# Slot numbers stored in a node's row, own places for rows, one-hots and staging, and x in host-laid tiles

## Chip, cores and metric

The kernel runs on one core of one Trainium2 chip. The metric is device time in microseconds (us) of that core for one launch, inputs in HBM. Times are medians of a kernel's runs. A ratio is the mean time of one kernel's runs over that of the kernel before in the same rounds, so it is not quite the ratio of the medians quoted beside it. There is one profile of each kernel, so marks and rates compared below are of single executions; only the times and ratios come from several.

## The reference, cut to what matters

Four graph layers run one after the other on x (8 batches, 2048 nodes, 64 features). The change concerns the first one, a hypergraph attention layer with 64 hyperedges, and one set of loads in the stage after it.

```python
def _L0_gnn_ref(x, H, adj, ...):
    h = x @ W
    alpha = softmax(where(H.T > 0, leaky_relu(h @ a_node), NEG))        # node -> hyperedge
    agg = einsum('ben,bnf->bef', alpha, h)                              # the 64-row "table"
    beta = sigmoid((h @ a_gn)[:, None, :] + (agg @ a_ge)[:, :, None])
    all_he = elu(beta[..., None] * h[:, None] + (1 - beta[..., None]) * agg[:, :, None])
    deg = maximum(adj.sum(-1), 1.0)[:, None]
    industry = einsum('nm,bmf->bnf', adj / deg, x @ W_ind)              # the products "u"
    coefs1 = softmax(where(H > 0, attn_scores(elu(agg)), NEG))          # hyperedge -> node
    g = einsum('bne,benf->bnf', coefs1, all_he)
    # ... g and industry are then combined, and three more layers follow
```

A node belongs to a few hyperedges only. The kernel sorts the nodes by that number and works in "slots": slot s of a row tile (128 sorted nodes) is each node's s-th hyperedge, picked from the table by a one-hot matmul.

## The kernel before: the parts concerned

Layer 0, in the program's order. Names: `hrow` is a gathered row, `hrh` and `hrl` are its two halves, `o` is a one-hot, `ps` holds the scores of a row tile's slots, from which VectorE makes the factors `R` and `co`; `pz` is row plus table entry of one slot, `du` are the degrees, `v0h` and `v0l` the halves of a piece of x. SyncE and ACT issue the loads and stores, GpSimd the gathers. The parts that the argument needs:

```python
def split(pool, src, tag, bufs, shape):          # f32 as two fp32r halves
    ...
    nc.scalar.copy(hi, src)
    nc.vector.tensor_tensor(lo, src, hi, ALU.subtract)

def load_adj(t):                                 # adj tile t: 2 x 512 KB
    for k in range(2):
        a = pa.tile([P, HN], F32, tag="a", name="a", bufs=4)
        nc.sync.dma_start(a, adj_t[t * P:(t + 1) * P, cols(k, HN)])
        if t < NT - XT: nc.gpsimd.tensor_copy(adj[t][:, cols(k, HN)], a)    # 12 tiles
        else:           nc.scalar.copy(adj[t][:, cols(k, HN)], a)           # the last 4
...
for t in range(NT):                              # rows of H in sorted order, for the slot numbers
    nc.gpsimd.indirect_dma_start(out=hs[:, t, :], in_=h_ne, in_offset=order[:, t])
# ... row tiles h -> hs_hbm (two staging rows), agg, degree passes du += ones.T @ adj[t],
# ... slot numbers from hs, table tab2, ts2; then all of adj is cast, then:

def begin(t):                                    # row tile t of the slot phase
    hrow = pl.tile([P, BF + 8], F32, tag="hrow", bufs=2)
    nc.gpsimd.indirect_dma_start(out=hrow, in_=hs_hbm, in_offset=order[:, t])
    both = split(pb, hrow[:, 0:BF], "hr", 2, [P, BF])
    # one-hots on GpSimd, ps matmuls, R, rs, co on VectorE
for t in range(NT):
    for s in range(S):
        # 3 matmuls into pz (PSUM); begin(t + 1) at s == 0
        fill(8)                                  # 8 of the 512 product matmuls "u"
        nc.vector.tensor_tensor(z, z, R[:, s], ALU.mult)                    # z lies in PSUM
        y = pl.tile([P, B, F], F32, tag="y", bufs=2)                        # y lies in SBUF
        nc.scalar.activation(y, z, AF.Exp, bias=-1.0)
        nc.vector.scalar_tensor_tensor(y, z, 1.0, y, op0=ALU.max, op1=ALU.min)
        nc.vector.tensor_tensor(y, y, cb, ALU.mult)                         # "y times co"
        nc.gpsimd.tensor_tensor(acc, acc, y, ALU.add)                       # s > 0
# inside the products, once: a block of 16 one-row matmuls "pdc" turns the degrees into a column
```

## Time and profile before

| | before |
|---|---|
| time, three runs | 2225.7 us median (2225.62 to 2230.62) |
| layer 0: start to the first gather of the next stage | 297.5 us |
| first row gather | 101.3 us |
| first product matmul | 112.6 us |
| last product matmul ends | 293.1 us |

The span splits at the next stage's first gather, which waits for layer 0's last product. Everything behind it is the same program in both kernels but for the loads of x.

### The profile page before, as it was taken

Reading aid. Unit: us, or ns where it says so; the run is one execution under the profiler, and the core shown is the slowest. Engines: PE = TensorE matmul, PEld = TensorE weight load, DVE = VectorE, ACT = ScalarE, POOL = GpSimd, SP = SyncE. Lnnn points to the kernel's source line nnn. Section 1 sums busy time; section 2 is a strip of 40 time slices with the busy share of each in tenths; the row PEclk is TensorE's granted clock in tenths of the full one; section 3 lists DMA queues with packets and bytes.
Section 4 is the critical chain, followed back from the end, with each engine's and each line's share of the span. In section 5 each row is a group of like instructions: output and inputs, shape, how many; then the busy total and the mean of one; then the engine's idle time right before and its main releaser. Section 6 shows DMA issues by size and latency. Waiting matters only on the chain.

```text
span 2227.2 us, 19810 instructions
## 1 busy us (share of the span) xinstructions
PE 1993.1 (89%) x7318; PEld 1289.3 (58%) x7318; DVE 1139.1 (51%) x1900; ACT 338.3 (15%) x584; POOL 551.0 (25%) x499
## 2 busy tenths in 40 slices
PE   7799978888759999799999999999986989999994
PEld 4488745555644444375456456447434777777873
DVE  5479956666532222216864773782784344331312
ACT  1322323222111111010010001001000011111110
POOL 5457466564323323200110110110010001010202
PEclk7889989999969999999999999999998999999997
DMA  8723334322210000000000000000001223200000
GB/s 263 237 66 91 95 91 107 83 70 63 76 46 0 19 19 19 19 24 5 10 5 3 10 8 1 10 8 3 8 8 32 76 72 85 62 19 1 20 1 21
DMA packets 99306, 103.26 MB, mean 46 GB/s; under 512 B 63088, under 2 KB 63136, under 8 KB 99008
## 3 DMA queue, kind: packets, MB, share of 16 engines
q1 hardware_dynamic: 73248, 83.09, 12.8%
q0 software_dynamic: 4064, 9.10, 1.7%
q10 hardware_dynamic: 21888, 9.70, 1.6%
q8 instruction: 60, 0.98, 0.2%
q14 instruction: 46, 0.38, 0.1%
HBM read 75.59 MB, written 26.28 MB: 46 GB/s over the span
## 4 chain that ended last, share of the span: by engine, by line
PE 63%; DVE 12%; DMA 12%; POOL 7%; issue 4%; ACT 2%; SPq 0%; ACTq 0%; POOLq 0%; DVEq 0%
PE py L967 18%; PE u L171 17%; PE u L914 10%; PE u L527 9%; DMA fcav<-in_adj_t 7%; POOL ln_r L155 3%; PE pz L171 2%; DVE fcav L1061 2%; PE pf L171 1%; PE pr L171 1%; DMA x<-x_hbm 1%; DVE ln_v L151 1%; DVE ln_c L145 1%; DVE ln_m L143 1%; ACT r L149 1%
## 5 line engine op out<-in xcount | busy, mean ns | idle before, releaser
L967 PE MATMUL py<-wp,xg 128*128 128x512 f32 x1024 | 448.5, 597 | 8.5 <-DVE fcav L972 5.8
L967 PEld LDWEIGHTS py<-wp,xg 128*128 128x128 f32 x1024 | 193.6, 191 | 254.4 <-issue 216.4
L171 PE MATMUL u<-adj,hi 128*128 128x512 f32 x768 | 256.5, 415 | 0.0
L171 PE MATMUL u<-adj,lo 128*128 128x512 f32 x768 | 246.5, 400 | 1.1 <-DVE lo L1026 1.1
L914 PE MATMUL u<-pt,xn 128*128 128x512 f32 x512 | 227.5, 603 | 8.3 <-DVE u L923 7.1
L972 DVE TENSOR_TENSOR fcav<-py,emb_n 128x512 f32<-128x512 f32 x256 | 177.0, 691 | 52.0 <-PE py L967 37.5
L975 POOL TENSOR_TENSOR r<-r,bias 128x256 f32<-128x256 f32 x32 | 23.3, 729 | 636.0 <-DVE r L973 636.0
L973 DVE TENSOR_REDUCE r<-fcav 128x32 f32<-128x512 f32 x256 | 175.4, 685 | 8.1
L914 PEld LDWEIGHTS u<-pt,xn 128*128 128x128 f32 x512 | 97.3, 193 | 130.2 <-issue 114.7
L527 PE MATMUL u<-adj,vh 128*128 128x512 f32 x512 | 158.3, 408 | 15.4 <-ACT vh L166 11.6
L171 PEld LDWEIGHTS u<-adj,hi 128*128 128x128 f32 x768 | 143.2, 190 | 40.8 <-issue 11.5
L171 PEld LDWEIGHTS u<-adj,lo 128*128 128x128 f32 x768 | 144.6, 190 | 35.4 <-DVE lo L1026 1.6
L527 PE MATMUL u<-adj,vl 128*128 128x512 f32 x512 | 152.1, 398 | 0.0
L155 POOL TENSOR_TENSOR ln_r<-ln_e,neg_half 128x8 f32<-128x8 f32 x64 | 106.1, 1658 | 174.9 <-DVE ln_e L153 166.9
L908 DVE TENSOR_SCALAR pt<-pt 128x512 f32<-128x512 f32 x64 | 49.1, 784 | 172.8 <-ACT pt L907 171.3
L1045 POOL TENSOR_TENSOR r<-r,xn 128x512 f32<-128x512 f32 x16 | 20.4, 1275 | 418.9 <-DVE r L1044 418.9
L527 PEld LDWEIGHTS u<-adj,vh 128*128 128x128 f32 x512 | 96.2, 189 | 45.7 <-ACT vh L166 13.1
L912 POOL TENSOR_TENSOR acc<-acc,pt 128x512 f32<-128x512 f32 x60 | 79.6, 1327 | 162.6 <-DVE pt L908 159.8
L527 PEld LDWEIGHTS u<-adj,vl 128*128 128x128 f32 x512 | 96.4, 189 | 22.1 <-issue 0.7
L1061 DVE SCALAR_TENSOR_TENSOR fcav<-fcav,adj 128x512 f32<-128x512 f32 x64 | 44.5, 695 | 117.6 <-DMA fcav<-in_adj_t 117.1
L149 ACT ACTIVATE r<-ln_c 128x512 f32<-128x512 f32 x64 | 40.4, 631 | 288.4 <-DVE ln_c L145 274.8
L709 POOL DMA_INDIRECT gn<-gs_hbm,rank x64 | 69.7, 1088 | 34.7 <-issue 14.2
(316 smaller groups left out, 2774.3 us busy)
## 6 DMA issues: line engine op xcount, KB each, us to landing
a<-in_adj_t SPq DMA_DIRECT2D x32, 512.0 KB, 5.9
fcav<-in_adj_t SPq DMA_DIRECT2D x64, 256.0 KB, 2.8
x_hbm<-r SPq DMA_DIRECT2D x20, 256.0 KB, 2.3
hs_hbm<-st ACTq DMA_DIRECT2D x16, 260.0 KB, 5.4
xt<-in_x_t SPq DMA_DIRECT2D x16, 256.0 KB, 5.4
u_hbm<-ut SPq DMA_DIRECT2D x16, 256.0 KB, 2.7
gs_hbm<-acc SPq DMA_DIRECT2D x16, 256.0 KB, 2.0
ut<-u_hbm SPq DMA_DIRECT2D x16, 256.0 KB, 3.2
```

Source lines behind the costliest of these rows:

```text
L149: nc.scalar.activation(r, xc, AF.Square)
L155: nc.gpsimd.tensor_tensor(rstd, vare, neg_half[:, :groups], ALU.pow)
L171: tc.keep_in_program_order(nc.tensor.matmul(*args, **kw))
L527: nc.tensor.matmul(u[c], lhsT=half[:, j, :], rhs=adj[t][:, cols(c)], start=t == 0 and i == 0, stop=ends and not own,)
L709: nc.gpsimd.indirect_dma_start(out=gn[:, j, :], out_offset=None, in_=g_rows, in_offset=bass.IndirectOffsetOnAxis(ap=rank4[:, p, c * JT + j ...
L908: nc.vector.tensor_scalar(pt, pt, 1.0, None, op0=ALU.max)
L912: nc.gpsimd.tensor_tensor(acc, acc, pt, ALU.add)
L914: nc.tensor.matmul(u[p], lhsT=xn[p][:, t, :], rhs=pt, start=t == 0, stop=t == NT - 1)
L967: nc.tensor.matmul(py.rearrange("p o d -> p (o d)"), lhsT=xg[b][:, q, cols(j, P)], rhs=wp[:, q, cols(k)], start=q == 0, stop=q == 1,)
L972: nc.vector.tensor_tensor(pr, py, e_b, ALU.mult)
L973: nc.vector.tensor_reduce(r[:, j, b, cols(k, OH)], pr, AX.X, ALU.add)
L1061: nc.vector.scalar_tensor_tensor(a, a, 1.0, adj[t][:, cols(k)].bitcast(F32), op0=ALU.mult, op1=ALU.not_equal, accum_out=left[:, t, k:k + 1],)
```

## The change

The intent: no gathers of H, for the slot numbers are computed in node order and travel as 64 more columns of each row; no waits of rows and reciprocals for adj's staging memory, for they get places of their own; row gathers after eleven of the sixteen adj tiles; the `lo` halves of x on GpSimd, to unload VectorE; and one x load where two with short pieces were. Cut to its core:

```diff
-    def split(pool, src, tag, bufs, shape):
+    def split(pool, src, tag, bufs, shape, eng=nc.vector):
-        nc.vector.tensor_tensor(lo, src, hi, ALU.subtract)
+        eng.tensor_tensor(lo, src, hi.bitcast(F32) if eng is nc.gpsimd else hi, ALU.subtract)
...
+    def staged(name):                            # shared by adj and x, four of 256 KB
+        return hy.tile([P, JT, P], F32, tag="x", name=name, bufs=4)
+    def load_adj(t):
+        for c in range(NCH):
+            a = staged("a").rearrange("p t f -> p (t f)")
+            nc.sync.dma_start(a, adj_t[t * P:(t + 1) * P, cols(c)])
+            tc.keep_in_program_order(nc.gpsimd.tensor_copy(adj[t][:, cols(c)], a))
...
+    HROW = BF + 8 + E
+    EARLY = 11
+        for c in range(NCH):                     # ahead of the small weights on ACT's queue
+            nc.scalar.dma_start(m_en[c], h_en[:, cols(c)])
-        for t in range(NT - XT):
+        for t in range(EARLY):
             load_adj(t)
...
+        # 16 small matmuls pcm, then the slot numbers of all nodes
+        nc.vector.tensor_tensor(slot, pcm, m_n, ALU.mult)
-        for t in range(NT):
-            nc.gpsimd.indirect_dma_start(out=hs[:, t, :], ..., in_=h_ne, ...)
...
-            st = pa.tile([P, BF + 8], F32, tag="st", name="st", bufs=2)
+            st = pa.tile([P, HROW], F32, tag="st", name="st", bufs=4)
+            nc.scalar.copy(st[:, BF + 8:], slot[:, t, :])
...
     def load_x(dst, p, c):
-        for b in range(2): ... eng.dma_start(dst[:, :, b * F:(b + 1) * F], x[2 * p + b, ...])
+        nc.sync.dma_start(dst, x_n[p, c])
...
-                part[c] = split(pb, xc.pop((p, c)), f"v{c}", 1, [P, JT, P])
+                part[c] = split(pb, xc.pop((p, c)), f"v{c}", 1, [P, JT, P], nc.gpsimd)
...
+        fetch_rows(0)                            # gathers; hrow in pool hy, three of them
+        fetch_rows(1)
+        for t in range(EARLY, EARLY + 2):
+            load_adj(t)
+        slots(0)                                 # pslot transpose, 12 one-hots on GpSimd
+        for t in range(EARLY + 2, NT):
+            load_adj(t)
         now = begin(0)
+        slots(1)
...
-                fill(8)
+                fill(4 if t == 0 and s < 6 else 8)
```

The last degree passes became filler between the slots of row tile 0, and products without slots follow at the end.

## The prediction

> **What bounds the kernel now.** I read the page first, then the chain of waits from 0 to 320 us, the waits from 60 to 140 us, the table of windows, and the timeline from 0 to 132 us and from 284 to 330 us. The change touches only layer 0 (0 to about 297 us) and, through the loads of x, the stage after it (297 to 640 us). The rest stands as it was, so the prediction is a sum over layer 0.
>
> Layer 0 has two halves. Until about 112 us the kernel loads adj (16.8 MB), computes rows and the one-hot table, and counts degrees. From 112 to 293.5 us TensorE runs 512 products `u` with 57 attention slots `pz` put between them. The chain of waits over the seam:
>
> ```profile
> 94.40 4.22 DMA a<-in_adj_t
> 98.65 1.04 ACT adj L253
> 99.69 0.92 ACT inv_row L505
> 100.61 0.70 issue
> 101.31 6.49 DMA hrow<-hs_hbm,order
> 107.84 2.04 DMA xc<-in_x
> 110.29 0.66 DVE R L630
> 111.58 1.24 PE pz L171 x2
> 113.44 0.69 DVE v0l L167
> 114.18 0.79 PE u L171
> ```
>
> The first row gather starts only at 101.31, when the last adj tile is cast and the degrees are copied, though the rows were written by about 79 us. Only then are rows gathered, x loaded, one-hots made and halves split, one after the other: 94 to 114 us is a string of waits. The waits from 60 to 140 us say the same:
>
> ```profile
> POOL hrow L613 <- ACT inv_row L505: 19.7, 1, 19.7
> DVE R L627 <- DMA xc<-in_x: 16.2, 1, 16.2
> ACT hrh L166 <- DMA hrow<-hs_hbm,order: 8.7, 2, 6.3
> ```
>
> GpSimd stands still for 19.7 us and VectorE for 16.2 us. (The releaser named for `R` is doubtful: the last `ps` matmul ends at 109.77 and `R` starts at 109.87.) The built program's wait lists explain it: the places of `hrow` and `R` are those of adj's staging buffers, so both wait for all eight last adj loads.
>
> The table of windows (us of the window, then PE, PEld, DVE, ACT, POOL busy, clock, DMA share, GB/s):
>
> ```profile
> 60.00:80.00 20.00, 15.22 (x60) 9.07 (x61) 15.01 (x35) 3.24 (x12) 12.29 (x12) 0.75 0.92 323
> 100.00:120.00 20.00, 13.56 (x35) 9.72 (x35) 8.17 (x21) 5.52 (x9) 14.04 (x22) 0.52 0.61 139
> 112.00:120.00 8.00, 7.47 (x20) 5.59 (x20) 6.10 (x15) 1.63 (x3) 4.38 (x6) 0.50 0.73 167
> 160.00:180.00 20.00, 20.00 (x91) 16.42 (x90) 19.85 (x39) 5.74 (x10) 13.31 (x14) 1.00 0.39 109
> 240.00:265.00 25.00, 21.45 (x95) 16.81 (x94) 24.96 (x46) 7.47 (x13) 9.56 (x8) 0.99 0.26 85
> ```
>
> Before 80 us the DMA engines are the bound (share 0.92 at 323 GB/s). From 160 us TensorE and VectorE are both full, and from 240 to 265 us VectorE alone is: TensorE has 3.6 us of gaps there.
>
> **What the Trainium skill says.** "DMA: Bandwidth & Descriptors", Anatomy of one DMA, gives a fixed cost of about 2 us a transfer that does not shrink with size. The trace agrees: the 256 KB loads of layer 3 land in 2.8 us (median). So half-size staging buffers, still four, hold less in flight. The same page, Specifications, wants at least 512 B a piece; here 63,088 of 99,306 packets are under that. "GPSIMD Engine Reference", section 3.1, puts a two-input elementwise operation on GpSimd at 1.96 times VectorE; here `acc` takes 1.294 us against 0.682, a factor of 1.9. "TensorE: Matmul & The Clock Gate", Part 1, says that the clock is halved after idling; here it is 0.50 from 112 to 120 us and eight `u` matmuls take 3.61 us, against 1.83 later.
>
> **The change, part by part.**
>
> Slot numbers. Gone are 16 gathers of H rows on GpSimd (median 0.96 us, 15.4 us, alternating with the adj casts between 32 and 52 us), VectorE's waits for them (9.9 us), 16 transposes, 4 ACT copies and 4 multiplies. In their place come 16 small matmuls and one multiply before row tile 0, which delay its matmuls to about 15 us (7.7 before), 64 columns more in each row, and a transpose and two ACT copies per tile later. The steady pace of row tiles was 2.2 us (`ex` at 31.49, 33.61, 35.86); before, it was lost to H waits and to the wait for the two staging rows (ACT 16.7 us behind `hs_hbm`). With four staging rows and no H gathers I take 2.2 us: the order is ready near 33 us as now, then 13 tiles, so the last row is issued at about 62 and lands near 67 us.
>
> adj. It now comes in 64 loads of 256 KB through four buffers, all cast on GpSimd (half of 1.04 us each). Estimate of the pace: 2.0 us fixed, 0.75 of transfer (256 KB at 350 GB/s, from the 70 to 80 us window, 351), 0.55 cast, 0.3 semaphores, with queueing 1.05 us a load, and 1.15 while rows are written. That is 4.2 to 4.7 us a tile. From the first at about 22 us, tile 10 is cast at about 70 us. The program places the first two row gathers after tile 10, so both conditions meet: gather at G = 69.
>
> From G on, by the order of the instructions on each engine: rows land at G+6.5; ACT takes them before it goes on with the table (`hrh` 0.62, `tab` 0.62, `hrh`, `het`), then `pf`, tanh, four degree passes' worth of tiles, `pse`, `ts`: table ready at G+14; one-hots 12 x 0.59 = 7.1 to G+22; first `z` on VectorE at G+23.6 = 92.6, against 112.84. But GpSimd casts tile 13 only after those 12 one-hots; then 5 more, tile 14 (its loads wait for the casts of 13), tile 15: cast at about G+33. Only then do the x loads get the four buffers: landed G+36. `v0h` on ACT, two row gathers and an `acc` go ahead on GpSimd, then `v0l` (1.3 us): G+38.4 = 107.4, against 114.2. Meanwhile 7 slots are done at VectorE's pace of 3 x 0.685 = 2.05 us, and the degrees run in their gaps.
>
> The products. TensorE's remaining work from there: 510 x 0.2287 = 116.6; 50 slots x 0.69 = 34.5; 40 `ps` at about 0.13 = 5.2; `pdc` 4.6, `pinv` 2.4, transposes 2.5; sum 165.8. Before it was 168 for 179.3 us of span; the difference was the cold clock (about 5.5 us until 129) and VectorE gaps (about 4.5). VectorE's remaining work after: 50 x 2.05 + 14 x 1.25 + 14 x 0.69 + 16 x 0.69 = 141 us, the 16 `lo` splits (11 us) having gone to GpSimd, which has some 125 us of work for this stretch. So TensorE alone is the bound; I add 2 us of gaps. End: 107.4 + 165.8 + 2 = 275.2, against 293.5: 18.3 us less. The tail is 59 products without slots; the next stage cannot start in it, because its first gather waits for the last product's store in both programs.
>
> x in host-laid tiles. 32 loads, in two pieces each with 256 B runs, become one each with 2 KB runs; ACT loses 16 issues of about 0.46 us in the next stage. DMA share there is 0.24 to 0.40 and the chain runs through arithmetic and waits on x1; I give it 1.5 us.
>
> Sum: 2225.7 - 18.3 - 1.5 = about 2206.
>
> **The rivals.** (1) The in-order queues give the gain back. GpSimd now carries every adj cast, the gathers and the one-hots, and the x buffers are adj's own. If adj comes at 5.3 us a tile (198 GB/s), tile 10 falls at 78 us, the first product at 116, and only the slots done early and the warmer clock are gained: about 2216. For it: only 1 MB in flight, and ACT's table work stands behind the gathers. Against it: the old H gathers are out of that queue. (2) VectorE stays the bound: then moving 11 us from it and starting 20 us earlier gives the whole 20 to 30 us, about 2198. For it: 19.85 of 20 us busy at 160 us; against it: its remaining 141 us lie well under TensorE's 166. (3) The transfers were hidden anyway: adj's bytes still set the first product and nothing moves, 2222. Against it: 94 to 114 us is a chain of latencies, not of bandwidth (139 GB/s from 100 to 120 us).
>
> **Range and chances.** The biggest doubts are G (plus or minus 6 us, one for one) and the gaps of the products (plus or minus 5). That gives 2195 to 2217 for 8 in 10. Faster by over 2% needs 2181, 25 us beyond my sum and some 44 us out of a stage with about 20 us of seam and 12 us of lost pace: 5%. Slower by over 2%: 1%.
>
> **What would show it.** Right: first row gather at 63 to 76 us; first `z` at 87 to 99; `v0l` of the first product at 101 to 114; last product at 268 to 283; VectorE below 90% between 160 and 240 us with TensorE full; no waits for `hs`. Wrong in step one if tile 10 is cast after 78 us; wrong in the handover if the gather is early and the product late; wrong in the pace if the span from the first to the last product is not 165 to 172 us; wrong in the last part if the stage from 297 to 640 us shifts by over 4 us against layer 0's end.

## More of the kernel before

One more line of the table of windows belongs here, because the prediction did not use it. Its columns are the window in us, its length, then busy time of TensorE, weight loads, VectorE, ACT and GpSimd (with counts), granted clock, DMA share and GB/s:

```profile
24.00:78.00 54.00, 41.41 (x187) 26.50 (x187) 34.08 (x90) 7.23 (x30) 37.02 (x37) 0.76 0.85 279
```

Over the whole stretch in which adj comes in and rows go out, the DMA engines moved 279 GB/s, less than the 323 GB/s of its last part.

## The result, and the profile after

The changed kernel takes 2236.55 us (2236.23 to 2237.39, 4 runs) against 2228.16 us (2225.62 to 2231.14, 4 runs) of the kernel before: ratio 1.0038, 95% interval 1.002 to 1.0055. It is slower by a little, within the 2% that count as the same, and outside the predicted range of 2195 to 2217.

| mark, us | before | predicted | after |
|---|---|---|---|
| first row gather | 101.31 | 69 | 80.97 |
| first z on VectorE | 112.84 | 92.6 | 104.40 |
| last adj tile cast | 99.7 | 102 | 114.6 |
| first product matmul | 112.6 | – | 118.8 |
| first product with v0l | 114.18 | 107.4 | 119.9 |
| last product matmul ends | 293.1 | 275.2 | 301.0 |
| next stage's first gather | 297.5 | – | 305.65 |
| end of span | 2227.2 | – | 2235.6 |

So the gather came 20 us earlier and the products began 6 us later. Behind layer 0 the two kernels took 1929.7 and 1929.95 us. The table of windows of the changed kernel, in the stretches that answer to those shown of before:

```profile
24.00:78.00 54.00, 42.34 (x214) 27.67 (x214) 35.53 (x101) 8.40 (x42) 25.50 (x42) 0.94 0.85 280
96.00:104.00 8.00, 5.62 (x16) 4.39 (x17) 1.16 (x4) 0.52 (x2) 7.22 (x14) 0.51 0.00 1
112.00:120.00 8.00, 7.65 (x30) 5.55 (x29) 5.28 (x9) 3.88 (x7) 6.50 (x8) 0.92 0.77 246
160.00:180.00 20.00, 19.59 (x91) 15.67 (x89) 18.51 (x31) 6.60 (x15) 14.40 (x14) 1.00 0.30 90
240.00:265.00 25.00, 21.74 (x97) 16.76 (x96) 24.59 (x46) 9.31 (x20) 16.34 (x16) 1.00 0.23 78
```

Three things are to be seen. From 24 to 78 us the DMA engines move 280 GB/s, as before. From 96 to 104 us they move next to nothing (1 GB/s), with three adj tiles not yet in place. And from 160 us VectorE is still at 93 to 98% although 11 us of work were taken from it, and TensorE has gaps again at 240 us.

The waits from 60 to 140 us (us in total, times, longest) answer to those of before; the chain that ended last has no piece in this stretch in this trace:

```profile
POOL adj L212 <- DMA a<-in_adj_t: 14.6, 12, 2.9
...
DVE R L647 <- PE ps L172: 9.1, 2, 7.8
ACT hrh L167 <- DMA hrow<-hs_hbm,order: 8.3, 2, 7.6
```

The 19.7 us that the gather waited for adj's end are gone, as intended, and `R` no longer waits for a load. In their place stand waits for adj's loads and for the `ps` matmuls, which wait for one-hots.

What GpSimd does in that DMA pause, from its timeline (start, length, line, operation, count, and in brackets the idle time before and what ended it):

```profile
80.97 1.05 POOL L616 DMA_INDIRECT hrow<-hs_hbm,order  x1 [0.28 <-DMA a<-in_adj_t]
...
88.46 2.58 POOL L212 CAST adj<-a 128x512 fp32r<-128x512 f32 x4 [2.88 <-DMA a<-in_adj_t]
95.35 7.02 POOL L633 TENSOR_SCALAR o<-slot 128x128 fp32r<-128x128 bf16 x12 [4.30 <-ACT slot L629]
102.43 2.29 POOL L212 CAST adj<-a 128x512 fp32r<-128x512 f32 x4
104.68 2.73 POOL L633 TENSOR_SCALAR o<-slot 128x128 fp32r<-128x128 bf16 x5
107.47 2.81 POOL L212 CAST adj<-a 128x512 fp32r<-128x512 f32 x4
111.15 1.24 POOL L212 CAST adj<-a 128x512 fp32r<-128x512 f32 x2 [0.87 <-DMA a<-in_adj_t]
113.38 1.27 POOL L212 CAST adj<-a 128x512 fp32r<-128x512 f32 x2 [0.98 <-DMA a<-in_adj_t]
```

It waits 4.3 us for the slot numbers of row tile 0, makes twelve one-hots in 7 us, and only then casts adj tiles 13 to 15. The four staging buffers are full meanwhile, so nothing is loaded.

VectorE's groups from 120 to 300 us (line, operation, shapes, count, busy us, mean ns, idle before), before and then after:

```profile
L654 DVE TENSOR_TENSOR pz<-pz,R 128x512 f32<-128x512 f32 x56 | 38.0, 685 | 0.5 <-PE pz L171 0.5
L663 DVE TENSOR_TENSOR y<-y,co 128x512 f32<-128x512 f32 x41 | 30.2, 744 | 0.1
L167 DVE TENSOR_TENSOR hrl<-hrow,hrh 128x512 fp32r<-128x512 f32 x14 | 12.3, 881 | 0.0
```

```profile
L694 DVE TENSOR_TENSOR y<-y,co 128x512 f32<-128x512 f32 x39 | 36.8, 946 | 0.5
L685 DVE TENSOR_TENSOR pz<-pz,R 128x512 f32<-128x512 f32 x51 | 34.9, 687 | 0.8 <-PE pz L172 0.8
L168 DVE TENSOR_TENSOR hrl<-hrow,hrh 128x512 fp32r<-128x512 f32 x14 | 15.5, 1109 | 0.0
```

The multiplication with one operand in PSUM (`pz`) stayed at 0.69 us. The one with both operands in SBUF went from 744 to 946 ns, `hrl` from 881 to 1109 ns. One instance, and what GpSimd did at the same time, from the two timelines:

```profile
120.53 3.60 DVE L694 TENSOR_TENSOR y<-y,co 128x512 f32<-128x512 f32 x1
```

```profile
119.78 1.28 POOL L695 TENSOR_TENSOR acc<-acc,y 128x512 f32<-128x512 f32 x1
121.03 1.29 POOL L168 TENSOR_TENSOR v1l<-xc,v1h 128x512 fp32r<-128x512 f32 x1
122.29 1.29 POOL L168 TENSOR_TENSOR v2l<-xc,v2h 128x512 fp32r<-128x512 f32 x1
```

VectorE's operation took 3.6 us and ended 0.5 us after GpSimd's third. I sorted the single y times co entries of the timeline from 118 to 302 us of the changed kernel by what GpSimd ran beside them (overlaps under 0.1 us not counted): 20 with nothing beside them took 684 ns on average, 15 that overlapped a two-input GpSimd operation took 1313 ns. For `pz` the same two classes took 688 and 687 ns.

### The profile page after: what moved, and what is told of

The parts are those of the page before. It is cut to its first block, busy times and chain, and to the rows that moved or that the text cites. A ratio compares the mean times of both kernels' runs of the same rounds, so it can differ in the third digit from the quotient of the medians.

```text
span 2235.6 us, 19857 instructions
## 1 busy us (share of the span) xinstructions
PE 1988.0 (89%) x7330; PEld 1282.7 (57%) x7330; DVE 1137.7 (51%) x1875; ACT 338.2 (15%) x620; POOL 564.8 (25%) x539
## 4 chain that ended last, share of the span: by engine, by line
PE 54%; DVE 10%; DMA 9%; POOL 7%; issue 4%; ACT 2%; SPq 0%; POOLq 0%; ACTq 0%; DVEq 0%
PE py L999 18%; PE u L172 12%; PE u L946 10%; PE u L524 9%; DMA fcav<-in_adj_t 7%; POOL ln_r L156 3%; DVE fcav L1093 2%; POOL gn L741 1%; PE pr L172 1%; DVE ln_c L146 1%; DVE ln_v L152 1%; DVE ln_m L144 1%; PE pf L172 1%; ACT r L150 1%; DMA x<-x_hbm 1%
## 5 line engine op out<-in xcount | busy, mean ns | idle before, releaser
L1007 POOL TENSOR_TENSOR r<-r,bias 128x256 f32<-128x256 f32 x32 | 23.4, 730 | 636.1 <-DVE r L1005 636.1
L946 PEld LDWEIGHTS u<-pt,xn 128*128 128x128 f32 x512 | 98.5, 195 | 131.9 <-issue 117.0
L741 POOL DMA_INDIRECT gn<-gs_hbm,rank x64 | 70.2, 1098 | 48.0 <-DMA bd_w<-in_w_t 16.3
```

The source lines that it names most:

```text
L741: nc.gpsimd.indirect_dma_start(out=gn[:, j, :], out_offset=None, in_=g_rows, in_offset=bass.IndirectOffsetOnAxis(ap=rank4[:, p, c * JT + j ...
L946: nc.tensor.matmul(u[p], lhsT=xn[p][:, t, :], rhs=pt, start=t == 0, stop=t == NT - 1)
```

## An account of the product stretch

To compare kernels I cut the stretch from the first to the last product matmul into 60 equal windows. "Idle" is the sum of window minus TensorE busy; "clock loss" is the sum of TensorE busy times (1 minus granted clock); "rest" is what remains.

| kernel | first, last product | stretch | idle up to 145 / after | clock loss | rest | VectorE busy |
|---|---|---|---|---|---|---|
| before | 112.6, 293.1 | 180.5 | 0.5 / 3.6 | 9.0 | 167.4 | 162.7 |
| after | 118.8, 301.0 | 182.2 | 2.9 / 7.3 | 3.1 | 168.8 | 157.4 |
| lo_vector | 114.9, 297.1 | 182.2 | 4.8 / 3.4 | 7.2 | 166.8 | 156.9 |
| y_psum | 118.8, 298.3 | 179.5 | 6.1 / 0.7 | 5.8 | 166.9 | 140.9 |
| weights_first | 113.4, 299.4 | 186.0 | 4.3 / 7.2 | 6.2 | 168.3 | 156.3 |
| stage8 | 112.2, 299.9 | 187.7 | 4.2 / 7.3 | 8.0 | 168.2 | 156.9 |
| half2 | 115.8, 301.9 | 186.1 | 4.9 / 7.6 | 5.8 | 167.9 | 151.1 |
| onehot_vector | 114.1, 294.7 | 180.6 | 1.6 / 7.5 | 3.1 | 168.4 | 153.6 |
| early8 | 120.8, 303.2 | 182.5 | 2.5 / 8.6 | 4.4 | 167.0 | 144.8 |
| pair | 114.9, 288.1 | 173.2 | 2.0 / 0.6 | 4.1 | 166.5 | 139.7 |
| combo1 | 112.3, 285.4 | 173.1 | 3.0 / 0.7 | 2.3 | 167.1 | 139.7 |
| combo2 | 109.3, 292.2 | 182.9 | 1.6 / 0.4 | 9.9 | 171.0 | 139.8 |
| combo3 | 110.5, 282.4 | 172.0 | 1.6 / 0.5 | 1.7 | 168.2 | 139.7 |
| combo3b | 107.9, 279.7 | 171.8 | 1.2 / 0.4 | 1.7 | 168.5 | 139.9 |
| combo5 | 110.2, 283.1 | 172.8 | 3.2 / 0.4 | 3.0 | 166.2 | 140.5 |
| before_y_psum | 107.0, 282.1 | 175.0 | 0.5 / 2.1 | 4.7 | 167.7 | 159.1 |
| xtiles_only | 111.0, 290.1 | 179.1 | 0.8 / 5.2 | 4.7 | 168.4 | 163.4 |

The rest lies within 166 to 171 us in all of them: it is TensorE's work at full clock. What differs is idle time and clock. The last product after minus before is 7.9 us, and it splits into 6.2 (later start), 6.1 (idle), minus 5.9 (clock) and 1.4 (rest). The clock's part is not safe: the three kernels that share the old layer 0 lost 9.0, 4.7 and 4.7 us to it, and changed kernels with one small edit 3.1 to 8.0. The idle time after 145 us is steady: 7.2 to 8.6 us in the six kernels with y in SBUF and `lo` on GpSimd, at most 0.7 in the seven changed kernels with the slot result in PSUM.

## Experiments

Theory: the gain was lost at three places. The DMA engines, not the latency of a load, set when the first gather can start. GpSimd's one queue, with gather, one-hots and adj casts in line, sets the first product. And VectorE's two-SBUF-operand work waits for GpSimd's. The rivals stand in each expectation. Every kernel below is derived from the changed one unless it is said otherwise, and all gave correct results.

**lo_vector**: the `lo` halves of x back on VectorE.

```diff
-    part[c] = split(pb, xc.pop((p, c)), f"v{c}", 1, [P, JT, P], nc.gpsimd)
+    part[c] = split(pb, xc.pop((p, c)), f"v{c}", 1, [P, JT, P])
```

> The changed kernel with the 16 lo halves of x back on VectorE; nothing else differs. Theory one (VectorE and GpSimd keep each other out when VectorE reads two operands from SBUF): the y times co products fall from a mean of 946 ns to 740 to 780 ns and hrl from 1109 to about 900 ns, VectorE gets about 11 us of lo work back and loses about as much waiting, so the time stays within 3 us of the changed kernel (2233 to 2240). Rival (the move did unload VectorE, the product stage is long for another reason): y times co stays near 946 ns and the kernel is 6 to 11 us slower, 2243 to 2248.

Measured: 2231.71 us, ratio to the kernel before 1.0011 (0.9992 to 1.003). From 120 to 300 us the y times co products took 753 ns on average (946 in the changed kernel, 857 in stage8, which also keeps that work on GpSimd), `hrl` 905 ns. VectorE's busy time in the stretch is 156.9 us, against 157.4 with that work on GpSimd: moving 16 subtractions away had gained it nothing. The rival falls. The time came out a little under the expected 2233, but its interval overlaps that of the changed kernel.

**y_psum**: the activated slot result stays in PSUM, so that y times co has one operand there.

```diff
-    nc.vector.scalar_tensor_tensor(y, z, 1.0, y, op0=ALU.max, op1=ALU.min)
+    nc.vector.scalar_tensor_tensor(z, z, 1.0, y, op0=ALU.max, op1=ALU.min)
...
-        nc.vector.tensor_tensor(y, y, cb, ALU.mult)          # and acc likewise for s == 0
+        nc.vector.tensor_tensor(y, z, cb, ALU.mult)
```

> The changed kernel with the activated slot result written back to its PSUM bank instead of to SBUF, so that y times co reads one operand from PSUM; no work is added or removed. Theory one: y times co falls from 946 ns to 680 to 700 ns with none above 0.8 us, VectorE's busy time from 120 to 300 us falls by 9 to 12 us, the stretch from first to last product goes from 181 to 171 to 175 us, time 2227 to 2230. Rival (the gaps of the product stage come from the order of the filler, not from these waits): the stretch and the time stay within 2 us.

Measured: 2233.87 us, ratio 1.0013 (0.9994 to 1.0032). Its group of VectorE, 120 to 300 us:

```profile
L694 DVE TENSOR_TENSOR y<-pz,co 128x512 f32<-128x512 f32 x39 | 26.5, 685 | 0.9
```

Same operation, same count, 946 to 685 ns, none above 0.7 us in the timeline. VectorE's time in the stretch fell by 16.5 us, and TensorE's idle time after 145 us from 7.3 to 0.7 us. So the waits are shown, and that they made those gaps. But the time stayed above the expected 2227 to 2230, and the stretch shrank by 2.7 us only, not by the 6 to 10 expected: the handover up to 145 us got 3.2 us more idle and 2.7 us more clock loss. In this profile the block of degree transposes waited 3.5 us for VectorE's y times co, which now frees the PSUM bank that it needs; that the longer hold of the bank is the cause is argued, not shown.

**weights_first**: the H loads behind the small weights on ACT's queue.

```diff
-        (m_en tiles and their four loads ahead of w0t, a2, bd66)
+        (the same lines behind the loads of bd66)
```

> The changed kernel with the four H-transposed loads issued behind the small weights on the same queue. Both theories: the first row tile's matmul moves from 18.2 to about 11 to 13 us, and the last row is issued 5 to 7 us earlier (67 to 69 us instead of 73.9). Theory A (the first row gather hangs on adj's loads alone): gather stays at 79 to 82 us and the time within 2 us. Theory B (it hangs on the rows): gather at 73 to 76 us, time 5 to 7 us less.

Measured: 2234.68 us, ratio 1.0023 (1.0005 to 1.0041). The first row tile's matmul came at 16.8 us, 1.3 us earlier and not 5 to 7: the order of these loads was not what made phase A late. Last row issued at 71.5, gather at 78.9, first product 113.4, last 299.4 us. Neither theory is decided by so small a shift.

**stage8**: eight staging buffers for the early tiles (four of them in the early pool; `inv_row` moved to a later pool to make room).

```diff
+            if t < EARLY and c % 2:
+                a = early.tile([P, C], F32, tag="a", name="a", bufs=4)
+            else:
                 a = staged("a").rearrange("p t f -> p (t f)")
```

> The changed kernel with eight staging buffers of 256 KB instead of four for the first eleven adj tiles (2 MB in flight instead of 1 MB). Theory A (too little in flight): 44 early loads go from 1.30 us to 1.05 to 1.15 us each, tile 10 is cast at 70 to 74 us, the gather then waits for the rows and starts at about 77 to 79 us, time 2 to 4 us less. Theory B (the DMA engines, at a busy share of 0.88 to 0.98 with pieces of 2 KB, are the bound): pace stays 1.25 to 1.30 us, gather 79 to 82 us, time within 2 us.

Measured: 2232.33 us, ratio 1.0006 (0.9985 to 1.0027). The engines moved 299 GB/s instead of 280, and the 44 early loads took (76.9 - 23.05)/44 = 1.22 us each instead of 1.30: between the two expectations. The gather started at 78.4 us, 1.5 us after tile 10, behind the rows.

But the edit did not put twice as much in flight. From 24 to 74 us there were 4.0 loads between issue and landing on average, against 3.5 in the changed kernel, for SyncE, which issues the loads, stood still behind the row stores. Its waits from 20 to 80 us, in the changed kernel and here:

```profile
SPq L211 <- DMA hs_hbm<-st: 1.0, 1, 1.0
```

```profile
SPq L214 <- DMA hs_hbm<-st: 32.9, 13, 7.0
```

In the built program loads and stores share eight completion semaphores: the load issued at 40.01 us has the one of the row stored at 33.78 us, which landed at 39.95, and the loads behind it in SyncE's queue waited too. So whether 2 MB in flight would have given the prediction's pace is not tested by this run. The same waits, 27 to 31 us, stand in all five combinations below, which have these buffers too. What is safe: the six profiles with this edit moved 292 to 309 GB/s, the six with four buffers and the same order of gathers 280 to 286; the three with the old layer 0 scatter from 279 to 308.

**half2**: early tiles in 512 KB loads through two buffers, again 1 MB in flight.

```diff
-        for c in range(NCH): ... 256 KB, four buffers
+        for k in range(2):   ... early.tile([P, 2 * C], F32, tag="a", name="a", bufs=2)   # t < EARLY
```

> The changed kernel with the first eleven adj tiles in 512 KB loads (4 KB a partition) through two buffers, so again 1 MB in flight: the length of the pieces changes, the amount in flight does not. Theory A (short pieces cost the DMA engines time): from 24 to 78 us more than 295 GB/s instead of 280 at the same busy share, first gather at 76 to 79 us. Theory B (the engines move about 280 GB/s of this mix whatever the piece, as in the kernel before with 279): 275 to 285 GB/s, gather 80 to 84 us, time within 3 us of the changed kernel.

Measured: 2238.64 us, ratio 1.0051 (1.0025 to 1.0077). The engines moved 272 GB/s: no help from longer pieces is seen. The run did not stay a clean one: the built program put the row gathers behind eight tiles instead of eleven, so the gather started at 73.25 us. That made it a first test of another step: a gather 7.7 us earlier, and yet the last adj cast at 115.1 and the last product at 301.9 us.

**early8**: that test on purpose.

```diff
-    EARLY = 11
+    EARLY = 8
...
-        some_degrees(2)
         pse = pps.tile([E, B], F32, tag="sm", name="pse", bufs=2)
```

> The changed kernel with the first two row gathers placed after eight adj tiles instead of eleven (and two tiles' degree passes moved behind the table, so that none runs ahead of its tile). The prediction counted the time of the first gather one for one. If so: gather at 74 to 77 us once the rows are written, first product 4 to 7 us earlier (112 to 115 us instead of 118.8), time 4 to 7 us less. Rival (the first product hangs on the last adj tile, which GpSimd casts behind the one-hots while the DMA engines idle, so an earlier gather only moves more tiles behind it): gather at 74 to 77 us too, but last adj cast at 112 to 116 us and first product at 116 to 120 us, time within 2 us.

Measured: 2238.81 us, ratio 1.0036 (1.0017 to 1.0055). Gather at 73.6 us, 7.4 us earlier than in the changed kernel; last adj cast at 119.9 and first product at 120.8 us, 5.3 and 2 us later. GpSimd's timeline shows why it is even worse than the rival had it:

```profile
73.61 1.05 POOL L615 DMA_INDIRECT hrow<-hs_hbm,order  x1 [8.67 <-DVE agg L460]
...
83.72 7.02 POOL L632 TENSOR_SCALAR o<-slot 128x128 fp32r<-128x128 bf16 x12
90.81 2.28 POOL L212 CAST adj<-a 128x512 fp32r<-128x512 f32 x4
```

The gather stands in line with the casts, so GpSimd idles 8.7 us until the rows are written, and more tiles are behind it then. (The releaser named is a VectorE instruction of the same moment; the last row was issued at 70.2 us and has to land first.) The step "one for one" falls for a gather that is only moved in the program.

**onehot_vector**: the twelve one-hots of row tile 0 on VectorE.

```diff
-                nc.gpsimd.tensor_scalar(o, slot, float(s + 1), None, op0=ALU.is_equal)
+                eng = nc.vector if t == 0 else nc.gpsimd
+                eng.tensor_scalar(o, slot, float(s + 1), None, op0=ALU.is_equal)
```

> The changed kernel with the twelve one-hots of row tile 0 made on VectorE, which is idle then, instead of on GpSimd. Theory (from the gather to the first product GpSimd's queue is the bound, because adj's last tiles are cast behind the one-hots while the DMA engines idle): gather unchanged at 80 to 81 us, first z at 97 to 100 us instead of 104.4, last adj cast at 104 to 108 us instead of 114, first product 7 to 10 us earlier, time 4 to 8 us less if TensorE's gaps do not grow. Rival (the wait for the table through ACT and TensorE is the bound there): first z and first product move less than 2 us.

Measured: 2230.19 us, ratio 1.0013 (0.9992 to 1.0034). Gather unchanged at 80.06, first z at 98.5, last adj cast at 105.6 (9 us earlier), first product at 114.1 us (4.7 earlier, not 7 to 10), last product at 294.7 us, 6.3 us earlier than in the changed kernel. What the first product waited for now:

```profile
114.13 0.74 PE L172 MATMUL ug<-adj,v0h 128*128 128x512 f32 x2 [1.04 <-ACT inv_row L559]
```

`v0l` was ready at 109.4 us, but TensorE ran degree passes and slots in turn until 113.1, and the products take the PSUM banks of the degrees (`du` and `ug` share a tag in the changed kernel), so ACT has to copy the degrees out first. Behind GpSimd's line stands a second one, which the prediction did not have (read from this trace; no run tests it alone). That GpSimd's line sets adj's last cast is shown: 105.6 and, in pair below, 107.1 us, against 109.3 to 119.9 in the seven other kernels above, which keep these one-hots on GpSimd. What that is worth at the end is not shown so well: 4.7 to 6.3 us in this profile, but lo_vector, weights_first and stage8 began their products at 114.9, 113.4 and 112.2 us without it, and the interval of the ratio overlaps that of the changed kernel.

**xtiles_only**: the kernel before with the x tiles alone.

```diff
-        for b in range(2): ... eng.dma_start(dst[:, :, b * F:(b + 1) * F], x[2 * p + b, ...])
+        nc.sync.dma_start(dst, x_n[p, c])
```

> The kernel before with nothing but x laid out in tiles by the host (one load with 2 KB pieces in place of two with 256 B pieces). As the prediction had it: 1.5 us less over the mix stage, ratio to the kernel before 0.9985 to 1.0000. Rival (short pieces did cost time near the seam at 110 us as well): 4 us less or more, ratio 0.998 or below.

Measured: 2229.28 us, ratio 1.0008 (0.9987 to 1.0029). No gain in the time; 4 us or more is excluded, 1.5 us is inside the interval. The marks say more. From the next stage's first gather to the first matmul behind that stage (`u<-pt,xn`) the kernel before took 376.3 us and before_y_psum, the other one with the old loads, 378.3; this kernel took 374.9, the changed one 373.2, and the other 13 with the new loads 368.5 to 375.0. So a gain of the predicted size in that stage is likely. The total hides it: what lies behind, the same program in all, took 1553.4 us in the profile of before, 1558.7 here and 1556.7 in the changed kernel.

**combo1**: y_psum, weights_first, stage8 and onehot_vector together.

> Four repairs at once: slot result in PSUM, H loads behind the small weights, eight staging buffers, tile 0's one-hots on VectorE. If they add up: gather at 75 to 78 us, first z at 93 to 96 us, first product at 104 to 107 us, last product at 277 to 284 us, time 2212 to 2220. Rival (VectorE, TensorE's low clock and the handover take it back): last product at 288 us or later, time 2223 or more.

Measured: 2219.54 us, ratio 0.9969 (0.9949 to 0.9989): faster than both kernels, though within the 2% that count as the same, as every run here is. First z at 95.6 as expected, but the gather at 79.0, first product at 112.3 and last at 285.4 us, each later than expected; the time lies at the upper end. The stretch is 173.1 us.

**pair**: onehot_vector and y_psum only.

> The changed kernel with two repairs only: slot result in PSUM and tile 0's one-hots on VectorE. If the other two repairs of the first combination (H loads behind the weights, eight staging buffers) matter little: last product at 284 to 289 us (285.4 with all four), time within 3 us of that combination, 2217 to 2223. Rival: they carry a good part of it, last product at 290 us or later, time 2225 or more. After 145 us TensorE's idle time should be below 1.5 us either way, against 7.3 us in the changed kernel.

Measured: 2224.89 us, ratio 0.9972 (0.9951 to 0.9992), stretch 173.2 us, last product at 288.1 us. Idle time after 145 us is 0.6 us. Set beside onehot_vector alone, the slot result in PSUM shortens the stretch by 7.4 us here, once the handover is out of the way. The time lies just above the expected 2217 to 2223. combo1's last product is 2.7 us earlier, one profile against one; the ratios of the two do not differ, so a use of loads and staging is not shown.

**combo2** and **combo3**: combo1 with a tile of its own for degree plus one (a write to the tile that GpSimd still read made VectorE wait 2.5 us); combo2 also spreads the 16 degree transposes, one behind each of 16 products.

```diff
-                            nc.vector.tensor_scalar(deg1, pdc, 1.0, None, op0=ALU.add)
-                            nc.gpsimd.tensor_tensor(dinv, deg1, neg_half[:, :NT], ALU.pow)
+                            nc.vector.tensor_scalar(deg0, pdc, 1.0, None, op0=ALU.add)
+                            nc.gpsimd.tensor_tensor(dinv, deg0, neg_half[:, :NT], ALU.pow)
```

> The first combination, with the 16 one-column transposes of the degrees spread one behind each of 16 products instead of in one block, and with a tile of its own for degree plus one, so that VectorE need not wait for the power on GpSimd. Theory (the block of tiny matmuls and the wait behind it cost TensorE a hole of 2.4 us and some 4 us of half clock): idle before 145 us from 3.0 to below 1.5 us, clock loss from 2.3 to below 1 us, stretch of products 173 to 168 to 171 us, time 2214 to 2218. Rival (the low clock follows from the time, not from the block): clock loss stays at 2 us or more, time 2217 to 2221.

> The first combination with only the tile of its own for degree plus one; the one-column transposes stay in one block. Theory: the hole of 2.4 us behind the block goes, the half clock behind it stays; stretch of products 170 to 172 us, time 1 to 3 us below the first combination, and 1 to 3 us above the one with spread transposes. Rival: no change against the first combination (2219.5), as the wait moves elsewhere.

Measured: combo2 2227.01 us, ratio 0.9983 (0.9959 to 1.0007); combo3 2219.55 us, ratio 0.9946 (0.9926 to 0.9966), the fastest so far against its own rounds, with a stretch of 172.0 us as expected, though its interval overlaps combo1's. My theory of the spread was wrong: combo2's first product came at 109.3 us, but its stretch was 182.9 us with 9.9 us of clock loss. The same window in combo2 and in combo3b (combo3 run again, see below), columns as above:

```profile
120.00:136.00 16.00, 15.38 (x38) 9.77 (x39) 2.87 (x5) 1.34 (x4) 5.29 (x8) 0.50 0.00 0
```

```profile
120.00:136.00 16.00, 15.36 (x73) 12.36 (x72) 10.71 (x18) 5.54 (x10) 11.11 (x12) 0.92 0.00 1
```

TensorE counts as busy for 15.4 of 16 us in both, but at a clock of 0.50 it did 38 matmuls, and at 0.92 it did 73. The one-row matmuls stood between the products from 115.5 to 135.9 us, and the clock was at half from about 119 to 139 us. That they cause it is not shown: in xtiles_only the block of one-row matmuls ran from 119.0 to 122.7 us, and the clock stayed full:

```profile
118.00:122.00 4.00, 4.00 (x32) 3.54 (x30) 1.38 (x3) 0.60 (x1) 0.54 (x1) 1.00 0.01 4
```

**before_y_psum**, **combo5**, **combo3b**: the kernel before with the slot result in PSUM; combo3 with full 128 by 128 transposes in place of the one-row matmuls; and combo3 once more.

> The kernel before with only the slot result left in PSUM. If the waits of VectorE behind GpSimd were already there and cost time: y times co from 744 to 685 ns, VectorE's idle-free stretch shorter, TensorE's idle time after 145 us from 3.6 to below 1.5 us, last product 2 to 4 us earlier than 293, ratio 0.998 to 0.999. If they came with the change: less than 1 us at the last product, ratio 1.000.

> The second combination's better sister (slot result in PSUM, H loads behind the weights, eight staging buffers, tile 0's one-hots on VectorE, a tile of its own for degree plus one), with the degrees turned into a column by 16 full transposes of 128 by 128 instead of 16 matmuls of one row. Theory (TensorE's clock falls to half behind work that uses almost none of the array): clock loss before 145 us from 1.7 to 9.9 us in the other runs to below 1.5 us, stretch of products 168 to 171 us, time 1 to 3 us below combo3b. Rival (the drop follows the pause between degrees and products, whatever stands there): clock loss 1.7 us or more, as in combo3b.

> combo3 once more, beside combo5 and on a chip shared with it. If its gain is no accident of one chip: ratio to the kernel before 0.993 to 0.997, last product at 281 to 286 us, clock loss before 145 us 1.5 to 4 us.

Measured, all against the same 11 runs of the kernel before: before_y_psum 2223.83 us, ratio 0.9971 (0.9952 to 0.999); combo5 2217.84 us, ratio 0.9934 (0.9916 to 0.9952); combo3b 2216.38 us, ratio 0.9935 (0.9922 to 0.9948). The kernel before had these waits too: y times co fell to 681 ns, and idle after 145 us from 3.6 to 2.1 us, not below the expected 1.5. (Its last product at 282 us is not all owed to this: its gather came at 95.8 instead of 101.3 us in that profile, by chance.) combo3's gain holds. combo5's clock loss was 3.0 us and not below combo3b's 1.7: the rival expectation holds, and no help from full transposes is seen (one profile each).

GpSimd's timeline in combo3b, where the kernel after had its pause:

```profile
87.74 1.29 POOL L215 CAST adj<-a 128x512 fp32r<-128x512 f32 x2 [0.93 <-DMA a<-in_adj_t]
90.51 1.26 POOL L215 CAST adj<-a 128x512 fp32r<-128x512 f32 x2 [1.47 <-DMA a<-in_adj_t]
92.41 1.07 POOL L639 TENSOR_SCALAR o<-slot 128x128 fp32r<-128x128 bf16 x2 [0.64 <-ACT slot L634]
...
99.42 0.61 POOL L215 CAST adj<-a 128x512 fp32r<-128x512 f32 x1 [1.34 <-DMA a<-in_adj_t]
```

The last cast now ends at 100.0 us and waits for adj's loads, not behind one-hots. The first product comes at 107.9 us, again right behind the copy of the degrees (106.8 to 107.8).

## Why the prediction was wrong, point by point

The prediction is 30 us below the result; against the kernel before it said minus 20 us and it is plus 8.4. Four terms make up 27 of these 28 us; the kernel before was itself 2.5 us slower in the rounds of the result than in the three runs that the prediction started from.

**The pace of adj and of the rows (12 us).** The step that failed is "queueing 1.05 us a load, and 1.15 while rows are written" with the last row at about 62 us. Measured: 1.30 us a load ((80.7 - 23.4)/44), last row issued at 73.9, gather at 80.97 instead of 69. The form of the sum was right: behind the first four, each load but one was issued within 0.1 us of the cast that freed its buffer, and 4.6 us from issue to landing (median) plus 0.6 of cast, over four buffers, is 1.30. The term that was too small is the time to landing: the prediction's pace leaves 3.7 to 4.1 us for it.

It could have been seen before. 44 loads of 256 KB and 16 rows of 292 KB are 16.3 MB, and to pass them between 22 and 69 us takes 347 GB/s, while the kernel before moved 279 over that stretch, and no profile over 309; with 280 GB/s the gather falls at about 80. The prediction had called the DMA engines the bound, and then added up latencies.

How much of the longer landing is the engines' own limit stays open: their busy share was 0.85, the best long stretch is 337 GB/s at a share of 0.99 (stage8, 50 to 78 us), and stage8 did not put more than 4.0 loads in flight. The section of the skill from which the prediction takes 2 us is about transfers that GpSimd issues; adj's come from SyncE, and only the 2.8 us of layer 3, less 0.75 of transfer, carry that figure here. The rows were late too: ACT waited 19.4 us in ten places for stores to land, in spite of four staging rows. The prediction's first rival had this part right; its 5.3 us a tile from 22 us on gives 80, not the 78 that it says.

**From the gather to the first product (0.5 us as a size, wrong in part as a cause).** Gather to first z took 23.4 us (23.6 predicted), to v0l's product 38.9 (38.4): the in-order reading of GpSimd's queue was right to half a us. In the result the gather's delay was passed on one for one (12.0 and 12.5 us), because adj's pace holds up both. It is not the gather's own time that counts: early8 has it 7.4 us earlier and the first product 2 us later. What counts is adj's last cast, and behind it the last degree pass and its copy out of PSUM. The prediction saw the casts queue up behind the one-hots and took it as given; it should have gone on to say that the DMA engines would idle meanwhile. onehot_vector has the last cast 9 us and the first product 4.7 us earlier. Two readings were a little off: the last row was issued at 76.9 us and landed at 82.6, so the rows were not written "by about 79 us", and the last product ended at 293.1, not 293.5.

**The pace of the products (13 us).** The step that failed is "TensorE alone is the bound; I add 2 us of gaps". The stretch from v0l's first product is 181 us, not 167.8. Of the 182.2 us from the very first product, TensorE's full-clock work is 168.8 instead of 165.8 (plus 3), gaps are 10.2 instead of 2 (plus 8), clock loss is 3.1 where the prediction had none (plus 3). VectorE was to have 141 us and to fall under 90%; it had 157.4 us and stood at 93% from 160 to 240. The 16 us are not work: y times co adds (946 - 684) x 39 = 10.2 and `hrl` (1109 - 684) x 14 = 6.0 us. With the slot result in PSUM, VectorE's time is 140.9, close to the 141 predicted. The clock lost less in this profile than in that of before, 3.1 us against 9.0, but two other profiles of the old layer 0 lost 4.7, so a gain from a warmer clock is not shown.

**x in host-laid tiles (1.5 us).** Nothing measurable in the time. In the stage itself 3.1 us less in the profile of the changed kernel, within the 4 us that the prediction allowed; the unchanged program behind took 3.3 us more in that profile, which no part of the change explains.

The slot numbers' own part held: no waits for H rows are left. That the phase before row tile 0 grew to 18.2 us, not 15, was due to the order of the small loads for 1.3 us at most (weights_first: 16.8).

Open: why TensorE's clock falls to half somewhere between 115 and 140 us in every version but xtiles_only. With the one-row matmuls spread out it stayed at half longer (one run); full transposes in their place did not remove the drop.

The change was not bad in itself. With one-hots of row tile 0 on VectorE, the slot result in PSUM, a tile of its own for degree plus one, deeper staging and the H loads behind the weights it is 0.65% faster than the kernel before (combo3b), while the kernel before with its own slot result in PSUM gains 0.3% in the same rounds; the two intervals do not overlap.

## What to carry to other kernels

When work is moved from one engine to another, ask first which operands lie in SBUF on both sides: VectorE's two-operand work waited for GpSimd's here (up to 3.6 us for 0.68 us of work), and an operand left in PSUM cured it without an instruction more. Check every predicted start against bytes over GB/s of the same stretch, not of its best part. After adding buffers, count what is in flight: the queue that issues the loads can stand still for another reason. And a milestone made earlier is worth nothing if it stands in the same in-order queue ahead of what the next stage really waits for.

## What the Trainium skill lacked or had wrong

- "SBUF — State Buffer", section Who interferes with whom, states that a VectorE instruction with two SBUF inputs contends with a GpSimd instruction that reads SBUF, and that the loser blocks for the whole instruction. It had it right, and the prediction did not look it up. Here: 684 ns alone, 1313 ns on average beside a two-input GpSimd operation, up to 3600 ns; 685 ns with one input in PSUM. The page draws no line between GpSimd operations that read one input and two; in the kernel before, 11 y times co products beside casts and one-hots, which read one, took 705 ns on average.
- "TensorE: Matmul & The Clock Gate", Part 1, ties the half clock to idling. In combo2 the clock was 0.50 from 120 to 136 us with TensorE counted busy for 15.38 of 16 us, one-row matmuls among the products. What the busy measure counts is not said in a way that would have foretold it, nor why in xtiles_only a block of such matmuls went at full clock.
- No page read for this gave a rate for loads and row stores together on one core: 257 to 309 GB/s from 24 to 78 us over the 17 profiles, and 4.6 us (median) from issue to landing of a 256 KB load with 3.5 of them in flight beside the row stores.
